# Mamba scan with a hand-written slot order: the z projection, its SiLU and a pooled product change slots

## The chip, the cores and the metric

The kernel runs on one core of a Trainium2 chip. The metric is the device time of one execution in microseconds (us). A core has five engines that run side by side, each with its own queue of instructions that it takes strictly in order: TensorE (PE in the profile: matrix products), VectorE (DVE), ScalarE (ACT: activation functions and copies), GpSimd (POOL) and SyncE (SP: here it only issues DMA transfers). They wait for one another through semaphores, so an instruction that waits also holds up everything that stands behind it on its engine.

## The reference

The kernel computes two layers over 4096 tokens of 256 channels: a convolution with attention, then a layer of a bidirectional Mamba, a small MLP and a mixture of experts. The change is in the Mamba. For each direction:

```
xz = einsum('bld,ed->ble', x, in_proj_w);  xc, z = split(xz, 2)
xc = silu(causal_conv(xc, K=4) + conv_b)
dt, B, C = split(xc @ x_proj_w)                 # 16, 16, 16
dt = softplus(dt @ dt_proj_w + dt_proj_b)
h[t] = exp(dt[t]*A) * h[t-1] + dt[t]*B[t]*xc[t]  # 512 channels x 16 states
y[t] = sum_states(h[t] * C[t]) + xc[t]*Dp
y = (y * silu(z)) @ out_proj_w
```

The two directions are added; then come a layer norm, an MLP with leaky ReLU and a second layer norm (in the kernel: the "tail").

## The kernel before

All four phases are in one program; the function `mamba_phase` holds the one at issue. Tokens are cut into 8 chunks of 512 (`NCH`), and each chunk is done in both directions: 16 iterations `i`, even ones forward, odd ones backward. `ET` = 4 blocks of 128 inner channels, and within each block the 16 states are four groups `k`, with 128 partitions holding 32 channels times 4 states. Two such tiles of 512 tokens make one slot (128 x 1024), so an iteration has 4 x 4 x 2 = 32 slots; `at` is the slot's number in it.

The order of every engine's instructions is the order in which the loop over `slots` at the end of `mamba_phase` emits them (`tc.manual_schedule`). Nothing is moved later. In slot n the loop emits:

- `inflow(n + 2)`: GpSimd multiplies dt*xc by B (L1928, tile `dbx`, three buffers). Its operands `dtxr` and `b` are spread over the partitions by DMAs that SyncE issues (`load_dt`, `load_bc`).
- `keep(n - 1)`: ScalarE copies the last column of slot n-1's scan into the state (L1977).
- `decay(n + 1)`: ScalarE computes exp(dt*A) into PSUM (L1918, tile `da`, two buffers), from the DMA'd tile `dtr`.
- `bring(n + 1)`: the carry, one column added to `dbx` (L1971 on ScalarE; in the slots of `LONG` L1969 on GpSimd). From iteration 2 on alone.
- `recur(n)`: VectorE's scan (L1941), in place in `da`, or into the tile `h` (four buffers) in the slots of `POOLED`.
- the product with C: by VectorE from `da` into `h` (`readout`, L1951), or, for a slot in `POOLED`, by GpSimd in place in `h`, emitted one slot later (`pooled`, L1956). Both follow the state's copy.
- `sum_states`: TensorE sums the states of two slots into `y` (L1986). It is emitted two slots after the pair's first one, or three where that is pooled. `h` of slot n is overwritten in slot n + 4, so this sum must be done by then.
- at slots 1, 9, 17 and 25 `close`: VectorE multiplies `y` by silu(z) (L1995).

Beside this the loop takes steps of generators, each a piece of other work between two `yield`s. `prepare(q)` makes the inputs of the next iteration, one step a slot: projections (slots 27 to 31), convolution as four tap products a block (slots 3 to 7), SiLU (slot 8), x projection `wx` (slot 9), dt projection `wdt` (slots 11 to 15), and softplus with a rounding term that TensorE adds up (`rounding`, `total`, `logs`, `keep_dt`; slots 17 to 26). The z half of the input projection is in it: `z_of` is two matrix products into one of two PSUM tiles `mm`, `keep_z` ScalarE's copy out of it. `output` is the output projection (slots 1 to 3). `tail(c)` is the layer norm, MLP and second layer norm of a finished chunk, whose 36 steps are taken in slots from 3 of an even iteration on; each step says which engine it needs next, and `FULL` names the slots in which that engine takes no step of the tail. Its layer norms pass a row through DMAs twice each, with SyncE waiting for the first before it issues the second (L138/L140 and L145/L146). Before the change the tail ends in slot 30 of the odd iteration.

SiLU is in another table of ScalarE than exp and log, so each SiLU has a table load before and after it.

Of the kernel before, what the change touches and what calls it, by code (L numbers as in the profile page):

```python
# [30 lines left out]
NCH = NT // N  # L31
# [6 lines left out]
ET = DI // P  # L38
# [1217 lines left out]
def mamba_phase(cx, early, w_in, w_x, w_out, w1, w2, x1d, ud, bcd, dtd, x2d, u2d, usum):  # L1256
# [12 lines left out]
    with ExitStack() as ctx:  # L1269
# [60 lines left out]
        def exp_and_log():  # L1330
            nc.scalar.preload_act_table_set("natural_log_exp_and_others")

        def mm_psum():
            return pmm.tile([P, N], FP, name="mm", tag="mm")
# [13 lines left out]
        def load_u(i):  # L1348
            c, d = divmod(i, 2)
            u = early.new_u()  # L1350
            nc.sync.dma_start(out=u, in_=ud[NCH - 1 - c if d else c])
            gots[i] = {"u": u}

        def in_pair(q, e):
            return [in_proj(q % 2, gots[q]["u"], e), in_proj(q % 2, gots[q]["u"], e + 1)]

        def few():
            return sp.tile([P, N], FP, name="few", tag="few", bufs=3)

        def prepare(q):  # L1360

            d, got = q % 2, gots[q]

            ps = in_pair(q, 0)
            yield
            yield
            xp = early.wide("xp")
            nc.scalar.copy(xp[:, :, 0:3], halo[d])
            for v in range(2):
                nc.scalar.copy(xp[:, v, 3:], ps[v])  # L1370
            ps = in_pair(q, 2)
            yield
            yield
            for v in range(2):
                nc.scalar.copy(xp[:, 2 + v, 3:], ps[v])
            nc.scalar.copy(halo[d], xp[:, :, N : N + 3])
            for _ in range(4):
                yield

            xc = None  # L1380
            for e in range(ET + 1):
                if e > 0:
                    xc = got["xc"] = xc or pr.tile([P, ET, N], FP, name="xc", tag="xc")
                    nc.scalar.activation(xc[:, e - 1, :], ps, AF.Identity, bias=cx.col(f"convb{d}", e - 1))
                if e < ET:
                    ps = mm_psum()
                    for k in range(4):
                        nc.tensor.matmul(  # L1388
                            ps, taps[d][:, 4 * e + k, :], xp[:, e, k : k + N], start=k == 0, stop=k == 3
                        )  # L1390
                yield
            nc.scalar.activation(xc, xc, AF.Silu)
            exp_and_log()
            yield
            ps = mm_psum()
            nx = DR + 2 * DS
            for e in range(ET):
                nc.tensor.matmul(ps[0:nx, :], wx[d][:, e, :], xc[:, e, :], start=e == 0, stop=e == ET - 1)
            z_of(q, 0)
            yield  # L1400
            xd = few()[0:nx, :]
            nc.scalar.copy(xd, ps[0:nx, :])
            keep_z(q, 0)
            z_of(q, 1)

            at = 0 if d else DR
            nc.sync.dma_start(out=bcd[q], in_=xd[at : at + 2 * DS, :])
            yield


            r = slice(32 * d, 32 * d + DR)
            ex = dt = None
            for e in range(ET + 1):
                if e == 0:
                    keep_z(q, 1)
                if e > 0:
                    ex = early.wide("ex")[:, :, 0:N] if e == 1 else ex
                    dt = got["dt"] = dt or sp.tile([P, ET, N], FP, name="dt", tag="dt")
                    nc.scalar.activation(ex[:, e - 1, :], ps, AF.Abs, bias=cx.col(f"dtb{d}", e - 1))
                    nc.scalar.activation(dt[:, e - 1, :], ps, AF.Relu, bias=cx.col(f"dtb{d}", e - 1))  # L1420
                if e < ET:
                    ps = mm_psum()
                    nc.tensor.matmul(ps, wdt[r, P * e : P * e + P], xd[r, :], start=True, stop=True)  # L1423
                yield

            nc.scalar.activation(ex, ex, AF.Exp, scale=-1.0)
            yield
            rds, sums = {}, {}

            def rounding(e):  # L1430
                rds[e] = few()
                nc.scalar.activation(rds[e], ex[:, e, :], AF.Identity, scale=-1.0, bias=-1.0)
                nc.scalar.add(rds[e], rds[e], 1.0)

            def total(e):
                sums[e] = mm_psum()
                for v, x in enumerate((rds.pop(e), ex[:, e, :], dt[:, e, :])):
                    nc.tensor.matmul(sums[e], cx.ident, x, start=v == 0, stop=False)  # L1438

            def logs(e):  # L1440
                nc.scalar.activation(ex[:, e, :], ex[:, e, :], AF.Ln, bias=1.0)

            def keep_dt(e):
                nc.scalar.copy(dt[:, e, :], sums[e])
                if q < 2:
                    return
                h = e // 2
                if e % 2 == 0:
                    firsts[q, h] = ip.tile([P, 2], FP, name="first", tag="first")
                nc.scalar.copy(firsts[q, h][:, e % 2 : e % 2 + 1], sums[e][:, 0:1])  # L1450
                if e % 2:
                    first_rows[q, h] = cx.rows.tile([P, 2], FP, name="first_row", tag="first_row", bufs=2)
                    nc.sync.dma_start(out=first_rows[q, h], in_=firsts[q, h])

            rounding(0)
            yield
            for e in range(ET + 1):
                if e > 0:
                    keep_dt(e - 1)
                if e < ET:  # L1460
                    total(e)
                if e < ET - 1:
                    rounding(e + 1)
                if 0 < e < 3:
                    keep_z(q, e + 1)
                yield
                if e < ET:
                    logs(e)
                    if e < 2:
                        z_of(q, e + 2)  # L1470
                    nc.tensor.matmul(sums[e], cx.ident, ex[:, e, :], start=False, stop=True)
                if e > 0:
                    dt_piece(q, 1, e - 1)
                if e == 1 and q + 1 < 2 * NCH:
                    load_u(q + 1)
                if e == ET and q > 1:
                    load_first(q, 0)
                yield

        def z_of(q, e):  # L1480
            zs[e] = in_proj(q % 2, gots[q]["u"], ET + e)

        def keep_z(q, e):
            if e % 2 == 0:
                gots[q].setdefault("z", []).append(sp.tile([P, 2, N], FP, name="z", tag="z", bufs=3))
            nc.scalar.copy(gots[q]["z"][e // 2][:, e % 2, :], zs.pop(e))
# [421 lines left out]
        gots, bcs, dts, m_of, das, us, ys, hs = {}, {}, {}, {}, {}, {}, {}, {}  # L1908
# [25 lines left out]
        def recur(n):  # L1934
# [3 lines left out]
            h = hs[n] = hp.tile([P, 2, N], FP, name="h", tag="h")  # L1938
            if n % SPS in POOLED:
                das[n] = h  # L1940
# [5 lines left out]
        def readout(n):  # L1946


            i, e, k, j = slots[n]
            if n % SPS not in POOLED:  # L1950
                nc.vector.tensor_tensor(hs[n], das[n], bcs[i, k][1][:, None, :].to_broadcast([P, 2, N]), ALU.mult)  # L1951

        def pooled(n):

            i, e, k, j = slots[n]
            nc.gpsimd.tensor_tensor(hs[n], hs[n], bcs[i, k][1][:, None, :].to_broadcast([P, 2, N]), ALU.mult)  # L1956
# [36 lines left out]
        def close(i, e):  # L1993
# [4 lines left out]
        CARRY = {30: (0, 0), 31: (0, 2), 9: (1, 0), 11: (1, 2)}  # L1998


        POOLED = {0, 4, 8, 12, 16, 20, 28}

        AHEAD = 5

# [1 line left out]
        LONG = {1, 9, 17, 24}  # L2006

        FULL = {
            "PE": {1, 2, 3, 4, 5, 6, 7, 9, 18, 20, 21, 22, 24, 27, 29},
            "ACT": {0, 6, 7, 8, 9, 14, 15, 16, 20, 22, 30, 31},  # L2010
            "POOL": {1, 5, 9, 13, 17, 21, 23, 25, 27, 29, 30, 31},
            "DVE": {8, 11, 16, 24},
            "DMA": {},
        }
        needs = ["PE"]
        with tc.manual_schedule(engines=ORDERED):
# [5 lines left out]
            for n, (i, e, k, j) in enumerate(slots):  # L2022
                at = n % SPS
# [12 lines left out]
                if nxt[0] < 2 * NCH:  # L2036
# [4 lines left out]
                    if (k, j) == (2, 2):  # L2041
                        load_dt(*nxt, 2)
                if n > 0 and (n - 1) % SPS in POOLED:
                    pooled(n - 1)
                if j == 2 and n > 2 and (n - 3) % SPS in POOLED:
                    sum_states(n - 3)
                if j == 0 and n > 0:
                    if (n - 2) % SPS not in POOLED:
                        sum_states(n - 2)
# [4 lines left out]
                if 1 <= at <= 3 and out is not None:  # L2054
                    step(out)
                    if at == 3:
                        out = None
                        if (i - 1) % 2:
                            tails.append(tail((i - 1) // 2))
                if at == 0 and i > 0:  # L2060
                    for z in gots[i]["z"]:
                        nc.scalar.activation(z, z, AF.Silu)
                    exp_and_log()
                if i == 0:
# [376 lines left out]
```

## Time and profile before

| what | value |
|---|---|
| median of 3 runs | 4107.07 us (4106.33 to 4110.94) |
| the profiled execution, its span | 4108.35 us, 4106.5 us |
| Mamba, start of iterations 2 and 14 | 2168.7 and 3584.2 us: 117.95 us an iteration |
| VectorE's scans, pooled ones, products (L1941, L1941, L1951) | 400 x 2347 ns, 112 x 2343 ns, 400 x 1221 ns |
| GpSimd's inflow and pooled products (L1928, L1956) | 512 x 2358 ns, 112 x 2357 ns |
| ScalarE's decay (L1918) | 1024 x 691 ns |
| z copy (L1486), z SiLU (L2062), a table load | 567, 1049, 1283 ns |
| mean granted TensorE clock | 0.935 |

A row of the profile's groups names the line, engine, operation and tiles (out<-in), how many there were, their busy time and mean duration, and then how long the engine sat idle before them and what ended that. In the view of waits a line reads "who <- for whom: total us, times, longest". In the timeline a row has its start, its length, the instruction and, in brackets, the idle time before it and its releaser. Instructions start a little before the one ahead has ended, so a plain slot takes VectorE 3.53 us and a pooled one 2.26.

### The profile page before, as it was taken

Reading aid. Unit: us, or ns where it says so; the run is one execution under the profiler, and the core shown is the slowest. Engines: PE = TensorE matmul, PEld = TensorE weight load, DVE = VectorE, ACT = ScalarE, POOL = GpSimd, SP = SyncE. Lnnn points to the kernel's source line nnn. Section 1 sums busy time; section 2 is a strip of 40 time slices with the busy share of each in tenths; the row PEclk is TensorE's granted clock in tenths of the full one; section 3 lists DMA queues with packets and bytes.
Section 4 is the critical chain, followed back from the end, with each engine's and each line's share of the span. In section 5 each row is a group of like instructions: output and inputs, shape, how many; then the busy total and the mean of one; then the engine's idle time right before and its main releaser. Section 6 shows DMA issues by size and latency. Waiting matters only on the chain. (4 is left out here: it accounts for less than half of the span.)

```text
span 4106.5 us, 43589 instructions
## 1 busy us (share of the span) xinstructions
PE 3577.7 (87%) x14968; PEld 1200.4 (29%) x14968; DVE 3456.2 (84%) x2887; ACT 2640.9 (64%) x4233; POOL 1814.7 (44%) x1193
## 2 busy tenths in 40 slices
PE   6769888999999999997788888888888988786898
PEld 2224332222222222222222223222322323222344
DVE  8998777989889889877899999998999999899322
ACT  1111226888888888875678777787877778775222
POOL 3020000000000000002888888888888889898100
PEclk9889998999999999998889999898999989897999
DMA  6232215223222323214333344434334334432121
GB/s 208 94 103 92 80 58 158 51 61 64 66 61 57 66 63 65 50 41 143 121 101 117 113 132 121 136 121 122 109 103 136 122 124 132 132 113 88 56 63 55
DMA packets 164325, 399.95 MB, mean 97 GB/s; under 512 B 36997, under 2 KB 46469, under 8 KB 163838
## 3 DMA queue, kind: packets, MB, share of 16 engines
q1 hardware_dynamic: 137166, 304.26, 23.9%
q0 software_dynamic: 24624, 84.43, 8.9%
q10 hardware_dynamic: 2304, 8.39, 0.6%
q8 instruction: 119, 1.95, 0.2%
q14 instruction: 112, 0.92, 0.1%
HBM read 268.17 MB, written 79.56 MB: 85 GB/s over the span
## 5 line engine op out<-in xcount | busy, mean ns | idle before, releaser
L1928 POOL TENSOR_TENSOR dbx<-dtxr,b 128x1024 f32<-128x1024 f32 x512 | 1202.6, 2358 | 225.5 <-DMA dtxr<-dtd 99.5
L1044 ACT ACTIVATE e<-sc 128x1024 f32<-128x1024 f32 x1024 | 993.7, 1023 | 165.5 <-PE sc L1037 143.0
L1941 DVE TENSOR_TENSOR_SCAN da<-da,state,dbx 128x1024 f32<-128x1024 f32 x400 | 938.9, 2347 | 58.5 <-ACT dbx L1971 17.4
L954 DVE TENSOR_TENSOR s<-s,e 128x1024 f32<-128x1024 f32 x768 | 880.2, 1216 | 19.7 <-ACT e L1044 19.0
L1918 ACT ACTIVATE da<-dtr,aneg 128x512 f32<-128x512 f32 x1024 | 707.9, 691 | 34.5 <-DMA dtr<-dtd 3.1
L1037 PE MATMUL sc<-q,kS 32*128 32x512 f32 x4096 | 648.7, 646 | 15.7 <-ACT e L1044 11.4
L961 PE MATMUL av<-e,vT 128*32 128x512 f32 x4096 | 551.8, 609 | 0.1
L1951 DVE TENSOR_TENSOR h<-da,c 128x1024 f32<-128x1024 f32 x400 | 488.5, 1221 | 22.9 <-PE mm L1423 1.4
L977 POOL DMA_DIRECT2D s<-s x94 | 81.5, 874 | 942.3 <-DVE s L954 856.8
L462 PE MATMUL cv<-v,u 128*128 128x512 f32 x928 | 413.5, 606 | 28.3 <-DVE pad L283 14.2
L1986 PE MATMUL y<-h,sel 128*32 128x512 f32 x2048 | 335.8, 629 | 95.0 <-DVE h L1951 77.2
L1037 PEld LDWEIGHTS sc<-q,kS 32*128 32x128 f32 x4096 | 211.0, 184 | 455.8 <-issue 254.0
L1941 DVE TENSOR_TENSOR_SCAN h<-da,state,dbx 128x1024 f32<-128x1024 f32 x112 | 262.5, 2343 | 53.6 <-PE y L1986 44.1
L1956 POOL TENSOR_TENSOR h<-h,c 128x1024 f32<-128x1024 f32 x112 | 263.9, 2357 | 28.9 <-ACT state L1977 28.8
L1342 PE MATMUL mm<-u,win 128*128 128x512 f32 x464 | 237.7, 654 | 30.7 <-ACT xp L1370 28.1
L462 PEld LDWEIGHTS cv<-v,u 128*128 128x128 f32 x928 | 179.1, 195 | 260.5 <-issue 228.1
L560 DVE SCALAR_TENSOR_TENSOR acc<-pad,wdw_s,acc 128x768 f32<-128x768 f32 (+1 forms) x192 | 235.9, 1233 | 19.9 <-ACT acc L553 14.2
L1977 ACT COPY state<-da 128x2 f32<-128x2 f32 x399 | 63.1, 158 | 280.8 <-DVE h L1951 279.4
L1388 PE MATMUL mm<-xp,taps 128*128 128x512 f32 x480 | 214.1, 598 | 0.0
L143 POOL TENSOR_TENSOR ln_few<-ln_few,minus_half 128x4 f32<-128x4 f32 x29 | 32.1, 1106 | 398.4 <-DMA ln_few<-ln_row 259.5
L954 DVE TENSOR_TENSOR s<-e 128x1024 f32<-128x1024 f32 x128 | 152.0, 1217 | 59.2 <-ACT e L1044 50.3
L961 PEld LDWEIGHTS av<-e,vT 128*32 128x32 f32 x4096 | 81.7, 108 | 394.4 <-issue 386.7
(381 smaller groups left out, 3910.8 us busy)
## 6 DMA issues: line engine op xcount, KB each, us to landing
dtr<-dtd SPq DMA_DIRECT2D x128, 512.0 KB
dtxr<-dtd SPq DMA_DIRECT2D x128, 512.0 KB
s<-s POOLq DMA_DIRECT2D x94, 512.0 KB, 6.0
b<-bcd SPq DMA_DIRECT2D x64, 256.0 KB
c<-bcd SPq DMA_DIRECT2D x64, 256.0 KB
dtd<-dt SPq DMA_DIRECT2D x64, 256.0 KB
dtd<-few SPq DMA_DIRECT2D x64, 256.0 KB
u<-uv SPq DMA_DIRECT2D x24, 640.0 KB
```

The costliest lines, as they stand in the source:

```text
L462: nc.tensor.matmul(rows4(ps), u[:, dy, P * ci : P * ci + P], v[:, dy : dy + HR, ci, :], start=dy + ci == 0, stop=dy == k - 1 and ci == CT - 1,
L954: nc.vector.tensor_tensor(z, x, y, ALU.add)
L961: nc.tensor.matmul(g.av[32 * h : 32 * h + 32, :], vT[:, kb, P * t + 32 * h : P * t + 32 * h + 32], es[h // 2][:, h % 2, :], start=kb == 0, ...
L1037: nc.tensor.matmul(ps[h // 2][:, h % 2, :], kS[r, t, P * kb : P * kb + P], q_t[r, t, :], start=True, stop=True,)
L1044: nc.scalar.activation(e, ps[i], AF.Exp)
L1342: nc.tensor.matmul(ps, win[d][:, t, P * e : P * e + P], u[:, t, ::-1] if d else u[:, t, :], start=t == 0, stop=t == CT - 1,)
L1918: nc.scalar.activation(da[:, v, :], dts[i, e, j][0][:, v, :], AF.Exp, scale=aneg[i % 2][:, a : a + 1])
L1928: nc.gpsimd.tensor_tensor(u, dts[i, e, j][1], bcs[i, k][0][:, None, :].to_broadcast([P, 2, N]), ALU.mult)
L1941: nc.vector.tensor_tensor_scan(das[n].rearrange("p v n -> p (v n)"), da.rearrange("p v n -> p (v n)"), u.rearrange("p v n -> p (v n)"), st ...
L1951: nc.vector.tensor_tensor(hs[n], das[n], bcs[i, k][1][:, None, :].to_broadcast([P, 2, N]), ALU.mult)
L1956: nc.gpsimd.tensor_tensor(hs[n], hs[n], bcs[i, k][1][:, None, :].to_broadcast([P, 2, N]), ALU.mult)
L1986: nc.tensor.matmul(ys[i, e][32 * j : 32 * j + 32, :], cx.sel, hs[n + j // 2][:, j % 2, :], start=False, stop=k == SQ - 1,)
```

## The change

The z products go from slots 9, 10, 19 and 21 to slots 15, 17, 19 and 21, the copies of them from slots 10, 11, 20 and 22 to slots 17, 18, 21 and 23, and the SiLU of z from slot 0 of the iteration that uses it to slot 28 of the one before. The rounding term of block 2 goes from slot 20 to 19. Slot 0's product with C goes to VectorE and slot 10's to GpSimd. The sets `FULL` change, which moves the steps of the tail: it now begins in slot 11 instead of 8, and ends in slot 4 of the next even iteration.

```
             for e in range(ET):
                 nc.tensor.matmul(ps[0:nx, :], wx[d][:, e, :], xc[:, e, :], start=e == 0, stop=e == ET - 1)
-            z_of(q, 0)
             yield
             xd = few()[0:nx, :]
             nc.scalar.copy(xd, ps[0:nx, :])
-            keep_z(q, 0)
-            z_of(q, 1)
...
-                if e == 0:
-                    keep_z(q, 1)
...
                     nc.tensor.matmul(ps, wdt[r, P * e : P * e + P], xd[r, :], start=True, stop=True)
+                else:
+                    z_of(q, 0)
                 yield
...
             rounding(0)
+            keep_z(q, 0)
+            z_of(q, 1)
             yield
...
-                if e < ET - 1:
+                if e == 0 or e == 2:
                     rounding(e + 1)
-                if 0 < e < 3:
-                    keep_z(q, e + 1)
+                if e == 0:
+                    keep_z(q, 1)
                 yield
                 if e < ET:
                     logs(e)
+                    if 0 < e < 3:
+                        keep_z(q, e + 1)
                     if e < 2:
                         z_of(q, e + 2)
                     nc.tensor.matmul(sums[e], cx.ident, ex[:, e, :], start=False, stop=True)
+                if e == 0:
+                    rounding(2)
...
-        POOLED = {0, 4, 8, 12, 16, 20, 28}
+        POOLED = {4, 8, 10, 12, 16, 20, 28}
...
-            "PE": {1, 2, 3, 4, 5, 6, 7, 9, 18, 20, 21, 22, 24, 27, 29},
-            "ACT": {0, 6, 7, 8, 9, 14, 15, 16, 20, 22, 30, 31},
-            "POOL": {1, 5, 9, 13, 17, 21, 23, 25, 27, 29, 30, 31},
-            "DVE": {8, 11, 16, 24},
+            "PE": {1, 2, 3, 4, 5, 6, 7, 8, 9, 10, 15, 18, 19, 20, 21, 22, 24, 27, 29},
+            "ACT": {6, 7, 8, 9, 16, 17, 18, 19, 22, 28, 29, 31},
+            "POOL": {5, 9, 11, 13, 17, 21, 23, 25, 27, 29, 30, 31},
+            "DVE": {1, 9, 11, 17, 25},
...
-                if at == 0 and i > 0:
-                    for z in gots[i]["z"]:
+                if at == 28 and i + 1 < 2 * NCH:
+                    for z in gots[i + 1]["z"]:
                         nc.scalar.activation(z, z, AF.Silu)
                     exp_and_log()
```

Where the steps of the tail stand, by iteration and slot (e: even, o: the odd one after, E: the even one after that):

| step | before | after |
|---|---|---|
| mean product, subtraction, square | e8, e9, e10 | e11, e12, e13 |
| row out (L138/L140), power and row back (L143 to L146) | e12, e15 | e15, e18 |
| residual sum L1581, copies of m L1578 | e13/e14, e14 and e17 | e16/e17, e17 and e20 |
| normalization L149 on GpSimd, scale L1584 | e19, e21 | e22, e23 |
| MLP, L1594 to L1600 (products on VectorE) | e25, e28, e30, o8 | e28, e31, o11, o13 |
| MLP, L1605 and L1610 | o8, o10, o12 | o13, o16, o23 |
| second norm: subtraction, square | o13, o17 | o24, o25 |
| second norm: row out, power and row back | o21, o24 | o27, E0 |
| second norm: normalization L149, sum L1617 | o28, o29 | E3, E4 |

## The prediction

> **What bounds it now.** First the page: the profiled execution took 4108.35 us around a span of 4106.5, 1.3 us over the median of the runs shown.
>
> ```profile
> PE 3577.7 (87%) x14968; PEld 1200.4 (29%) x14968; DVE 3456.2 (84%) x2887; ACT 2640.9 (64%) x4233; POOL 1814.7 (44%) x1193
> ```
>
> Shares over the whole span mix four phases, so I then cut the Mamba phase into its iterations, an odd and an even one shown here (columns: stretch, us, then busy time of PE, PEld, DVE, ACT, POOL):
>
> ```profile
> 2755.00:2877.40 122.40, 99.93 (x288) 34.13 (x288) 109.66 (x68) 88.92 (x182) 101.75 (x58) 0.90 0.39 119
> 2877.40:2992.50 115.10, 100.38 (x296) 34.55 (x296) 109.34 (x69) 91.42 (x186) 101.04 (x58) 0.96 0.43 124
> ```
>
> VectorE works 109.5 us in each; what is left is its waiting. An odd iteration and the even one take 14.25 us of it, from the view of VectorE's waits over iterations 2 to 13 (six pairs):
>
> ```profile
> DVE h L1941 <- PE y L1986: 35.4, 18, 5.9
> DVE da L1941 <- ACT dbx L1971: 17.4, 18, 1.8
> DVE da L1941 <- ACT state L1977: 11.5, 11, 1.8
> DVE da L1941 <- POOL dbx L1969: 8.1, 5, 2.6
> DVE usum L1617 <- POOL u L149: 5.5, 6, 1.7
> ```
>
> So the change can save 14 us a pair at most. Third, the timeline tells where those waits sit. I write s8 for slot 8 and put its zero at the start of its scan. In s0 ScalarE's z SiLU holds up the decay of s2:
>
> ```profile
> 2756.75 1.28 ACT L2062 ACT_TABLE_LOAD   x1
> 2758.05 2.00 ACT L2062 ACTIVATE z<-z 128x1024 f32<-128x1024 f32 x2
> 2760.07 1.28 ACT L1331 ACT_TABLE_LOAD   x1
> ...
> 2761.46 1.41 ACT L1918 ACTIVATE da<-dtr,aneg 128x512 f32<-128x512 f32 x2
> 2762.81 0.28 ACT L1971 ACTIVATE dbx<-dbx,brought 128x1 f32<-128x1 f32 x1
> ```
>
> From load to carry's end it is 6.37 us, while s0 and s1 give VectorE 6.5 (2.26 pooled, 3.53 plain, 0.59 for the gate L1995). The worst stall is s12 of odd iterations: its scan overwrites the tile that TensorE must first sum for s8, and that sum stands behind two z projections and the tail's L1605 products:
>
> ```profile
> 2795.64 3.70 PE L1342 MATMUL mm<-u,win 128*128 128x512 f32 x8
> 2799.18 1.88 PE L1605 MATMUL tl<-a1a,w2s 128*128 128x512 f32 x4
> 2800.89 1.88 PE L1605 MATMUL tl<-a1b,w2s 128*128 128x512 f32 x4
> ...
> 2803.56 1.06 PE L1986 MATMUL y<-h,sel 128*32 128x512 f32 x8
> ```
> ```profile
> 2804.73 2.35 DVE L1941 TENSOR_TENSOR_SCAN h<-da,state,dbx 128x1024 f32<-128x1024 f32 x1 [5.88 <-PE y L1986]
> ```
>
> Last, TensorE after idling. The same 128x512 half-products that start every 0.43 us in the rows above start every 0.85 here:
>
> ```profile
> 2941.31 2.08 PE L1438 MATMUL mm<-few,ident 128*128 128x512 f32 x2 [5.21 <-ACT few L1433]
> 2943.18 1.91 PE L1438 MATMUL mm<-ex,ident 128*128 128x512 f32 x2
> ```
>
> **The change part by part.** No operation is added or dropped: VectorE keeps 25 products of 1.22 and 32 scans of 2.35 an iteration, GpSimd 7 products of 2.36. All is in the waits, so I rebuild them by stretch, per pair.
>
> *s8 to s16: z projections and copies leave s9 to s11; s10 becomes pooled.* ScalarE in s8: keep and decay of s9 end at 1.7, two table loads and the 1.91 us SiLU at 6.2, keep of s8, decay and carry of s10 at 8.0. VectorE is there after 2.26 + 3.53 + 0.59 = 6.4: s10 waits 1.64. Today the tail's sums cover part of that (0.73 at s8 in odd, 1.21 at s9 in even iterations); the new FULL sets move them to s11 and s12. TensorE then runs wx from 4.9 to at most 10.5 (half speed), skip 0.9, sum of s8 0.9: done 12.3, and s12 is due at 13.8, so **the wait at s12 goes**. GpSimd: its carry step waited 4.06 us on ScalarE, itself behind the z copy; now it runs at 11.5, then the input of s13 to 13.9, the new product of s10 to 16.2, input of s14 to 18.6, s15 to 21.0, product of s12 to 23.3, input of s16 to 25.7. Due: s13 16.1, s14 19.6, s16 26.6. Covered, by a microsecond only at s14 and s16. At s8 itself the even wait goes (the sum reduction, now in s4, gives TensorE 1.14 more); in odd iterations s0 to s2 lose today's waits, four tap products of 3.45 us finish late, and s8 waits 0.65. Waits: even 1.65, odd 2.25. Today 0.49 + 0.58 + 2.01 + 0.11 = 3.2 in each on average.
>
> *s28 to s3: the z SiLU.* The same chain starts 1.95 after s28: the carry of s30 ends at 1.95 + 6.37 = 8.32, VectorE is ready at 2.26 + 3.53 = 5.79, or 6.43 where the tail puts a 0.73 product in s28 (even). So s30 waits 2.53 odd and 1.89 even: it is the old stall of s2 in a new place, and larger, since s1 had the 0.59 gate. At s0 nothing is pooled or loaded any more, so s1 and s2 lose their 0.67 and 1.19, and the reduction's 0.46 wait on GpSimd at s29 goes (it stands after GpSimd's normalization in s4). One new debt: SyncE's dtr load of s29 waits for the decay of s30, now at 8.0 instead of about 5.0, and dtxr queues behind it. Issue at 9.1, 5.5 us to the data where few transfers are under way (s21 of iteration 7), 8.7 at this boundary in iteration 3: it lands between 14.6 and 17.9, the input of s1 is ready 2.6 later, and VectorE asks at 18.9 (odd) or 19.5. Waits from 0 to 1.6; I take 0.3 after odd and 0 after even iterations, since part of that delay is backlog which now drains while SyncE waits. Waits: 1.89 + 2.53 + 0.3 = 4.7 a pair; today 2.3 an iteration.
>
> *s17 to s25: z copies behind the rounding terms.* The rounding pair is 1.27, a copy 0.57. In odd iterations z's second projection and the tail keep TensorE busy until the sums begin, and s13, s16, s23, s24 carry tail work on VectorE; TensorE ends the sum of s16 11.5 after s17, which s20 wants at 11.1, and ScalarE stays ahead of s21 to s25: 0.4 to 0.5 in place of about 1.9 (0.56 at s20, 0.75 at s22, 0.74 at s24 in iteration 7). In even ones the tail's residual sum (L1581) now needs a copy of m that stands in s17 after rounding and z copy: ScalarE ends it 5.1 after s17. TensorE has been idle since 2.2, so the four half-products start slow: 3.6, then the total (0.85 + 5 x 0.43 = 3.0), skip and sum of s16 1.8: 13.6 against 11.0 at which s20 is due. **A new wait of about 2.5 at s20**; had TensorE stayed fast, 0.3. From there ScalarE is the chain: beside its 1.8 a slot for state, decay and carry it has the third rounding and logs in s22 and s23 behind the copy of dt, which waits for TensorE's z product, which waits for the z copy of s21. It ends dt's copy 24.1 after s17, rounding 25.3, the decay of s24 26.8, due 26.5; then logs 0.6, z copy 0.6 and the tail's scale 1.5 put the carry of s25 at 31.1, due 30.4. So 0.4 at s24 and 0.7 at s25. Even 3.6, today about 0.9.
>
> *Tail and its transfers.* The tail now crosses into s4 of the next even iteration; two blocking pairs of DMAs (a row out and back, 2.7 to 3.7 us each on SyncE) move from s12/s15 to s15/s18 and from s21/s24 to s27/s0. At s27 the 3.5 us are over before the load of s29 may start anyway; at s0 the next load is needed 12 us later. Nothing, then; up to 1.0 a pair if not.
>
> *Sum per pair:* 1.65 + 2.25 + 4.7 + 0.5 + 3.6 = 12.7, against 14.25: 1.55 less. Seven pairs, 10.9 us; iterations 0 and 1, with no tail, I hold even. 4108.35 - 10.9 - 1.3 for the median: **4096 us**.
>
> [...] In this trace 11 of 14 gaps of 2.0 to 3.0 us are followed by products at half pace (2.29 us before the L1605 product at 2786.83). [...]
>
> **Rivals.**
> *Faster, 4070 to 4090.* TensorE stays fast at s17 and the ScalarE load of s19 to s25 fits: 12.7 - 2.2 - 1.1 = 9.4 a pair, 34 us less than now, 4073. For it: the z projections fill time in which TensorE was idle. Against: the gaps above.
> *Slower, 4111 to 4120.* The SiLU in s28 delays the dtr/dtxr pair, and s1 waits for it in every iteration. It begins at a landing 16.3 after s28 (odd) or 16.9 (even), that is 7.2 and 7.8 after issue; in iterations 3 and 7 it took 8.7 and 7.8. Each microsecond beyond costs two a pair. At 8.7: 1.5 odd, 0.9 even, less the 0.3 counted, 2.1 a pair, 15 us: 4111. Since b and c of s28 now stand right ahead of it instead of 3 us earlier, 9.4 is possible: 3.5 a pair, 24 us: 4120. For it: SyncE's waits on ScalarE; against: nothing else is issued while SyncE waits, so the backlog drains.
> *GpSimd falls behind* at s14 or s16, with three products in s8, s10 and s12: its margins there are 1.0 and 0.9. In s14 of iteration 7 it waited 0.55 for dtxr; 2 to 3 us of such waits an iteration cost 1 to 2, 14 to 28 in all, from 4110 to 4124.
> *No change:* waits only change place; 4099 to 4115.
>
> **Numbers.** Noise is about 0.2%, 8 us. Chances: the sum above with a gain that can be told, 4085 to 4099, 0.30; faster rival 0.17; no change 0.15; slower by transfers 0.22; by GpSimd or an unlisted wait, 0.16. Bounds: the best of all terms is 9 a pair (4070), the worst adds longer half pace (0.6), late transfers (3.5) and a stall as large as today's at s12 (4.0): 20.8 a pair, 4153. A waits-only sum can also miss by a microsecond or two a pair either way, so I reach to 4062 below and, giving up the case of all ills at once, to 4140 above; the likeliest case alone spans 4085 to 4105.
>
> **What would show it.** Right: VectorE busy 109.5 still; s12's wait on L1986 near zero; a wait of 1.9 to 2.5 on ScalarE before s30; 1.0 to 1.7 before s10 in every iteration; about 2.5 on L1986 before s20 in even iterations alone. Wrong: a wait on GpSimd before s1 over 1 us, or GpSimd waiting for dtxr past the start of s0; waits at s13 to s16; the row of TensorE at s17 at full pace.

## The result, and the profile after

The changed kernel takes 4134.60 us (median of 4 runs, 4127.74 to 4138.24) against 4109.00 us before: a ratio of 1.0061, 95% interval 1.0043 to 1.0078. It is slower, by 25 us. The forecast was 4096 us, 11 us faster. The profiled execution took 4132.73 us around a span of 4130.9, 24.4 us more than that of before.

The page's line of engine totals of the changed kernel shows the same amount of work on VectorE (3456.6 against 3456.2 us):

```profile
PE 3606.7 (87%) x14968; PEld 1198.1 (29%) x14968; DVE 3456.6 (84%) x2887; ACT 2643.6 (64%) x4233; POOL 1820.7 (44%) x1193
```

The stretches of an odd and an even iteration of the changed kernel (the columns are those of the prediction's table: stretch, length, busy time of PE, PEld, DVE, ACT, POOL, clock, DMA share, GB/s):

```profile
2769.95:2887.86 117.91, 100.20 (x306) 33.83 (x300) 108.69 (x67) 90.59 (x185) 97.50 (x56) 0.94 0.36 115
2887.86:3008.83 120.97, 102.25 (x284) 33.62 (x284) 110.33 (x69) 90.47 (x184) 103.28 (x59) 0.89 0.40 122
```

The odd iteration got shorter (122.40 to 117.91 us), the even one longer (115.10 to 120.97); the pair went from 237.5 to 238.9 us here, and over iterations 2 to 13 from 117.95 to 119.39 us an iteration. VectorE is as busy as before, so all of this is waiting. Its waits in iterations 2 to 13 of the changed kernel (total us, times, longest; its lines stand three further down, so the scan is L1944, the carry L1974, the decay L1921 and the sum L1989):

```profile
DVE da L1944 <- ACT dbx L1974: 47.7, 30, 2.4
DVE h L1944 <- ACT state L1980: 19.0, 12, 1.7
DVE h L1944 <- PE y L1989: 17.0, 7, 2.6
DVE da L1944 <- ACT da L1921: 9.2, 6, 1.5
DVE m L1564 <- PE mm L1557: 5.9, 6, 1.0
DVE ln_xc L129 <- PE tl L122: 4.1, 12, 0.4
```

With two lines of 0.8 us together that is 103.7 us, 17.3 a pair, against 14.25 before and 12.7 forecast. Three more a pair, six times, are 18 of the 24 us that the two profiled executions differ by. Iterations 14 and 15 add 2.0, and 0 and 1 take 2.6 less: the Mamba phase, from its first scan to its last, is 17 us longer. The other 8 us lie ahead of it and behind it, where nothing was edited; over the twelve traces of this case the last activation of the attention ends between 1879 and 1893 us. The waits on TensorE's sums have halved (35.4 to 17.0); those on ScalarE's carries (`dbx`) went from 17.4 to 47.7, 30 times in place of 18. Eighteen of the 30 were in the forecast: s30 in every iteration and s25 in the even ones. The other twelve are s5 and s21 of the odd iterations, 1.70 us each, and with them go six waits of 1.54 us on a decay (`da` L1921), at s17 of the even ones. (Before, VectorE also waited six times for a decay, but 0.7 us, and at s24 of odd iterations.)

What holds ScalarE up there stands in the page's own groups. The decay's row, first before, then after (busy, mean ns, idle time of ScalarE in front of it, and what ended most of that):

```profile
L1918 ACT ACTIVATE da<-dtr,aneg 128x512 f32<-128x512 f32 x1024 | 707.9, 691 | 34.5 <-DMA dtr<-dtd 3.1
```
```profile
L1921 ACT ACTIVATE da<-dtr,aneg 128x512 f32<-128x512 f32 x1024 | 708.2, 692 | 74.6 <-DVE h L1944 43.5
```

ScalarE's decays now wait 43.5 us for a scan of VectorE, the scan of a pooled slot. The timeline of ScalarE at s16 to s18 of iteration 8 shows one of these waits:

```profile
2947.08 0.16 ACT L1980 COPY state<-da 128x2 f32<-128x2 f32 x1
2949.39 1.42 ACT L1921 ACTIVATE da<-dtr,aneg 128x512 f32<-128x512 f32 x2 [2.15 <-DVE h L1944]
2950.74 1.90 ACT L1423 ACTIVATE ex<-ex 128x2048 f32<-128x2048 f32 x1
...
2955.80 0.59 ACT L1581 COPY m<-tl 128x512 f32<-128x512 f32 x1
```

and VectorE's timeline in the same place:

```profile
2947.01 2.35 DVE L1944 TENSOR_TENSOR_SCAN h<-da,state,dbx 128x1024 f32<-128x1024 f32 x1
2950.89 2.36 DVE L1944 TENSOR_TENSOR_SCAN da<-da,state,dbx 128x1024 f32<-128x1024 f32 x1 [1.54 <-ACT da L1921]
```

The decay of s17 starts when the scan of s16 ends (2947.01 + 2.35 = 2949.36), not a slot ahead of it. VectorE must then wait out the whole decay: 1.42 us, or 1.70 where the carry (0.28) follows on ScalarE. The decay of s21 in iteration 7, where the carry is on ScalarE, and the scan that waits for it:

```profile
2843.42 1.42 ACT L1921 ACTIVATE da<-dtr,aneg 128x512 f32<-128x512 f32 x2 [2.10 <-DVE h L1944]
```
```profile
2845.08 2.36 DVE L1944 TENSOR_TENSOR_SCAN da<-da,state,dbx 128x1024 f32<-128x1024 f32 x1 [1.70 <-ACT dbx L1974]
```

That is what happens when a slot and the one before it have the same buffer. The two built programs list the PSUM bank of every tile, and there it stands: `da` has two buffers, and they are not handed out by turns. In the changed program s17 of even iterations and s5 and s21 of odd ones get the buffer of the slot directly before, in iterations 2 to 14 (7 times s17, 6 times s5 and s21), and so do five slots of iteration 0; in the program of before that happens in iteration 0 alone (s9, s13, s17). All of these slots follow a pooled one.

### The profile page after: what moved, and what is told of

Read it like the earlier page. It is cut to its first block, busy times and chain, and to the rows that moved or that the text cites. A ratio compares the mean times of both kernels' runs of the same rounds, so it can differ in the third digit from the quotient of the medians.

```text
span 4130.9 us, 43570 instructions
## 1 busy us (share of the span) xinstructions
PE 3606.7 (87%) x14968; PEld 1198.1 (29%) x14968; DVE 3456.6 (84%) x2887; ACT 2643.6 (64%) x4233; POOL 1820.7 (44%) x1193
## 5 line engine op out<-in xcount | busy, mean ns | idle before, releaser
L1944 DVE TENSOR_TENSOR_SCAN da<-da,state,dbx 128x1024 f32<-128x1024 f32 x400 | 939.0, 2348 | 79.1 <-ACT dbx L1974 48.1
L1921 ACT ACTIVATE da<-dtr,aneg 128x512 f32<-128x512 f32 x1024 | 708.2, 692 | 74.6 <-DVE h L1944 43.5
L1989 PE MATMUL y<-h,sel 128*32 128x512 f32 x2048 | 309.0, 637 | 35.5 <-POOL h L1959 21.5
L1342 PE MATMUL mm<-u,win 128*128 128x512 f32 x464 | 254.8, 689 | 92.8 <-ACT xp L1370 84.4
L1944 DVE TENSOR_TENSOR_SCAN h<-da,state,dbx 128x1024 f32<-128x1024 f32 x112 | 262.5, 2344 | 44.3 <-PE y L1989 21.7
L143 POOL TENSOR_TENSOR ln_few<-ln_few,minus_half 128x4 f32<-128x4 f32 x29 | 37.1, 1278 | 396.3 <-DMA ln_few<-ln_row 285.5
```

The lines of the kernel that those rows point to most:

```text
L1342: nc.tensor.matmul(ps, win[d][:, t, P * e : P * e + P], u[:, t, ::-1] if d else u[:, t, :], start=t == 0, stop=t == CT - 1,)
L1921: nc.scalar.activation(da[:, v, :], dts[i, e, j][0][:, v, :], AF.Exp, scale=aneg[i % 2][:, a : a + 1])
L1944: nc.vector.tensor_tensor_scan(das[n].rearrange("p v n -> p (v n)"), da.rearrange("p v n -> p (v n)"), u.rearrange("p v n -> p (v n)"), st ...
L1989: nc.tensor.matmul(ys[i, e][32 * j : 32 * j + 32, :], cx.sel, hs[n + j // 2][:, j % 2, :], start=False, stop=k == SQ - 1,)
```

## The experiments

The first theory: the shared buffers cost the three waits, and most of what follows them; without them the change gains about what was forecast. Rivals: the waits come from the moved work itself (ScalarE has too much to do in s17), or from the SiLU in s28, or from TensorE's half pace alone. Times on different chips are compared through the ratio to the kernel before on the same chip; 0.001 of it is 4.1 us.

**The buffers by turns, in the changed kernel and in the kernel before.** Two tags of one buffer each in place of one tag of two (two more tiles, outside the slots, get one of the two tags):

```
-        pda = ctx.enter_context(tc.tile_pool(name="c_pda", bufs=2, space=PSUM))
+        pda = ctx.enter_context(tc.tile_pool(name="c_pda", bufs=1, space=PSUM))
...
-            da = das[n] = pda.tile([P, 2, N], FP, name="da", tag="da")
+            da = das[n] = pda.tile([P, 2, N], FP, name="da", tag=f"da{n % 2}")
```

> The changed kernel with one edit: the tile da, in two buffers of one tag, becomes two tags of one buffer, taken in turn by even and odd slots. In the changed kernel the decays of s17 (even), s5 and s21 (odd) were given the PSUM buffer of the slot just before them, so that they had to wait for that slot's scan; in the kernel before this happens in iteration 0 alone. Theory: these three waits (1.54 + 1.70 + 1.70 = 4.94 us a pair of iterations) are what the prediction missed; they go, nothing else moves, and seven pairs give 35 us: about 4100 us, a ratio of 0.997 to 0.999 to before. Rival: ScalarE is late in these slots anyway (it has 3.3 to 3.9 us of work in each of s13 to s15); then the waits stay at 1 us or more and the time at 4125 to 4135.

> The kernel before with the same edit. It had shared buffers at s9, s13 and s17 of iteration 0 alone. Theory: no more than 0 to 4 us faster, 4103 to 4109 us. Rival, that taking turns by itself helps every iteration: over 10 us faster.

Measured: the changed kernel with buffers by turns 4095.28 us, ratio 0.9957 (0.9942 to 0.9973); the kernel before with them 4112.96 us, 0.9997 (0.9982 to 1.0013). So the edit is worth 0.0104, 43 us, in the one and nothing that can be told in the other. In the first, the decay's row and VectorE's waits of iterations 2 to 13 read:

```profile
L1921 ACT ACTIVATE da<-dtr,aneg 128x512 f32<-128x512 f32 x1024 | 708.2, 692 | 32.8 <-DMA dtr<-dtd 3.2
```
```profile
DVE da L1944 <- ACT dbx L1974: 27.3, 18, 2.4
DVE h L1944 <- ACT state L1980: 15.4, 12, 1.5
DVE h L1944 <- PE y L1989: 15.2, 13, 2.2
```

The idle time on the scan is gone, and so are the waits at s5, s17 and s21: 18 carries are left, and no wait on a decay. All waits come to 66.3 us, 11.05 a pair. The wait of s20 in even iterations fell too, from 2.65 to 0.53 us in five of six; a new one of 1.52 us came at s8 in odd iterations. The scan of s20 in iteration 8, in the changed kernel and with buffers by turns:

```profile
2964.66 2.35 DVE L1944 TENSOR_TENSOR_SCAN h<-da,state,dbx 128x1024 f32<-128x1024 f32 x1 [2.65 <-PE y L1989]
```
```profile
2946.35 2.35 DVE L1944 TENSOR_TENSOR_SCAN h<-da,state,dbx 128x1024 f32<-128x1024 f32 x1 [0.53 <-PE y L1989]
```

The theory stands, and against the rivals: the moved work and the SiLU in s28 are all still there, and the three waits are gone.

**TensorE's half pace at s17.** In the changed kernel TensorE idles there until ScalarE's copy of m (2955.80 above), and then works at half pace (two half-products take 1.88 in place of 1.12 us; the trace's record of the granted clock has 0.5 from 0.23 us after their start on, for 3.41 us):

```profile
2956.44 1.88 PE L1584 MATMUL tl<-m,ident 128*128 128x512 f32 x2 [3.01 <-ACT m L1581]
2958.12 1.91 PE L1585 MATMUL tl<-x,ident 128*128 128x512 f32 x2
2959.83 1.16 PE L1435 MATMUL mm<-few,ident 128*128 128x512 f32 x2
```

To see what that costs by itself, the z product of s17 is issued twice in even iterations, which fills 1.7 us of the idle time. The first run has that on top of the buffers by turns, the second on the changed kernel as it is:

```
             z_of(q, 1)
+            if d:
+                for t in range(CT):
+                    nc.tensor.matmul(
+                        zs[1], win[d][:, t, P * (ET + 1) : P * (ET + 2)], gots[q]["u"][:, t, ::-1],
+                        start=t == 0, stop=t == CT - 1,
+                    )
             yield
```

> The first kernel with, in even iterations, the second z product issued twice (the same result written again), which fills 1.7 of the 3.0 us in which TensorE idles in s17. Theory, that the wait before s20 of even iterations (2.65) comes from half-pace products after that gap: the residual sum and the total run at full pace, the wait falls to 0.3 to 0.6, 14 to 16 us in seven pairs. Rival, that the order alone makes it (the copy of m ends 5.1 after s17 and 6 us of work stand ahead of the sum of s16): it stays over 2 us and the time within 4 us of the first kernel.

> The changed kernel with its shared buffers left as they are, and the second z product of s16 issued twice in even iterations, so that TensorE has no 3.0 us gap before the third one at s17. The output is as before. If half pace after that gap makes the wait of s20 (the 3.0 us gap in the profile, then matmuls of 1.03 to 1.06 us), the wait of s20 in even iterations goes from 2.65 us to 0.3 to 0.8 us, and the time from 4134.6 us to 4117 to 4122 us (8 even iterations by some 2 us). If the third product is late because ScalarE frees its input late (the shared buffer at s17), whatever TensorE's pace, the wait stays above 2 us and the time within 5 us of 4134.6.

Measured: on top of the buffers by turns 4088.49 us, 0.9944 (0.9921 to 0.9967), which can't be told from 0.9957: with the buffers by turns alone the gap was already 1.1 to 1.7 us in five of six even iterations, and the pace full, so there was little to win. On the changed kernel 4118.45 us, 1.0020 (1.0005 to 1.0035), against 1.0061: 17 us, the time that the clock's theory had. (Lines behind 1454 stand six further down in both.) In iteration 8 of that run the gap is shorter and the products run at full pace, though ScalarE is held up at s17 as before:

```profile
2947.42 1.13 PE L1590 MATMUL tl<-m,ident 128*128 128x512 f32 x2 [2.58 <-ACT state L1986]
2948.38 1.02 PE L1591 MATMUL tl<-x,ident 128*128 128x512 f32 x2
```
```profile
2953.93 2.35 DVE L1950 TENSOR_TENSOR_SCAN h<-da,state,dbx 128x1024 f32<-128x1024 f32 x1 [0.95 <-PE y L1995]
```

s20 waits 0.95 in four of six even iterations. In the other two the gap was 2.89 us; the products began at full pace, the granted clock fell to half 1.2 and 1.4 us later, and s20 waited 2.65 again. So TensorE's pace at s17 costs 17 us by the medians; the Mamba phases of the two traces differ by 11.

What the shared buffers cost as a whole adds up from the waits in iterations 2 to 13. The changed kernel waits 17.3 us a pair, the one with buffers by turns 11.05. Of these 6.2, 4.94 are the three waits, 1.8 the wait of s20, 0.6 that of s10 in odd iterations and 0.4 the tail's subtraction, and the wait of s8 takes back 1.5. Six pairs make 37 us; the Mamba phases of the two traces differ by 41, the medians by 43.

**The SiLU back in slot 0**, with the buffers by turns:

```
-                if at == 28 and i + 1 < 2 * NCH:
-                    for z in gots[i + 1]["z"]:
+                if at == 0 and i > 0:
+                    for z in gots[i]["z"]:
```

> The first kernel of this call with the z SiLU back in slot 0 of the iteration that uses it. Theory (a stall is the ScalarE chain less VectorE's work in two slots): the waits before s30 (2.41 odd, 1.75 even) go; in s0, which is no longer pooled, VectorE has 3.53 + 3.53 + 0.59 = 7.65 against a chain that ends at 1.7 + 6.37 = 8.1 to 8.3, so s2 waits 0.4 to 0.7. About 1.5 us an iteration less, 22 us: 4075 to 4082. Rival: the stall of 2 us simply comes back at s2, as before the change (1.2 to 1.8): within 8 us of the first kernel.

Measured: 4071.49 us, 0.9891 (0.9864 to 0.9918). It beats both kernels, by somewhat more than expected, and no version measured is clearly faster. The 0.0066 to the version with the SiLU in s28 is 27 us; the Mamba phases of the two traces differ by 15. VectorE's largest waits in it are

```profile
DVE h L1944 <- ACT state L1980: 16.4, 13, 1.6
DVE da L1944 <- POOL dbx L1972: 11.5, 7, 3.4
DVE h L1944 <- PE y L1989: 10.4, 11, 2.2
```

The wait of s30 is gone; s1 now waits 0.96 us an iteration for GpSimd and s2 0.54 for ScalarE. With a product for VectorE to do in slot 0, the chain of SiLU and decay is nearly covered there: 56.7 us of waits in iterations 2 to 13 against 66.3. That is 1.6 a pair, so the waits explain less than half of the 27.

**The SiLU in slot 28 as the only part of the change**, in the kernel before with buffers by turns (the diff above in reverse).

> The kernel before with the two buffers of da by turns, and of the change only this: the SiLU of z in slot 28 of the iteration before in place of slot 0. Theory: the wait at s2 (1.38 us an iteration) goes, and one of about 2 us comes at s30, because ScalarE's 2.6 us of SiLU and of loading its table stand before the products of s29 and s30, which gives 0.3 to 0.6 us an iteration and a time of 4115 to 4122 us against 4113 us without the edit. Rival: ScalarE has less to do in s28 to s30 without the other moves of the change, the wait at s30 is under 1 us, and the edit by itself gains, 4100 us or less.

Measured: 4133.30 us, 1.0061 (1.0043 to 1.0078). The sign is the theory's, the size is three times the most that it allowed (9 us): 0.0064 over the control, 26 us, as much as in the changed kernel. (The Mamba phases of the two traces differ by 14 us.) Waits of iterations 2 to 13 in it:

```profile
DVE h L1941 <- PE y L1986: 56.8, 30, 4.3
DVE da L1941 <- ACT dbx L1971: 19.6, 21, 1.8
```

In the control they are 34.2 and 17.0. The wait at s30 is 1.11 us an iteration, less than expected; but VectorE now waits 0.76 at s0 and 1.37 at s8 for TensorE's sums (0 and 0.19 in the control). At s0 it is the SiLU again: ScalarE's copy of `xp` stands behind it, TensorE waits for that copy, and then takes 6.63 us for eight products of the projection, which took 3.60 in the control, ahead of the sum that s0 needs (iteration 6, before s0 of iteration 7):

```profile
2756.42 6.63 PE L1342 MATMUL mm<-u,win 128*128 128x512 f32 x8 [3.90 <-ACT xp L1370]
```

At s8 VectorE, no longer held at s1 and s2, comes before the sum is there. What was won at s1 and s2 (1.77 to 0.37) is waited for again at s0 and s8.

**Slot 10's product in place of slot 0's as the only part**, in the same control.

```
-        POOLED = {0, 4, 8, 12, 16, 20, 28}
+        POOLED = {4, 8, 10, 12, 16, 20, 28}
```

> The kernel before with the two buffers of da by turns, and of the change only this: slot 10's product on GpSimd in place of slot 0's. First theory: the waits of s1 and s2 of before (0.39 and 1.38 us an iteration) mostly go, since s0 and s1 then take 7.64 us against a chain of about 8.1 us, and the wait at s12 or s10 grows by some 1.3 us in the odd iterations, which leaves about 1.3 us a pair, and a time of about 4100 us against 4113 us without the edit. Rival: what is won at s1 and s2 is all waited for again at s10 to s12, and the time stays at 4108 to 4118 us.

Measured: 4128.83 us, 1.0047 (1.0032 to 1.0062): slower by 20 us than the control (17 in the Mamba phases of the traces), which neither theory had. s1 and s2 gave back 1.2 us an iteration, as expected; but s12 of odd iterations waits 7.09 us (3.65 in the control). TensorE and VectorE at s9 to s12 of iteration 7 in it:

```profile
2799.13 2.85 PE L1605 MATMUL tl<-a1a,w2s 128*128 128x512 f32 x4 [2.29 <-DVE a1b L1600]
2801.77 2.75 PE L1605 MATMUL tl<-a1b,w2s 128*128 128x512 f32 x4
...
2808.02 3.70 PE L1342 MATMUL mm<-u,win 128*128 128x512 f32 x8
```
```profile
2817.11 2.35 DVE L1941 TENSOR_TENSOR_SCAN h<-da,state,dbx 128x1024 f32<-128x1024 f32 x1 [7.09 <-PE y L1986]
```

VectorE now asks for s12 1.1 us sooner after s10, and TensorE is later: behind a gap of 2.29 us (1.85 in the control) the eight L1605 products run at a lower pace, 5.4 us for 3.7.

**The z products, rounding terms, copies and the tail's places alone**: buffers by turns, SiLU in slot 0, slot 0's product on GpSimd again (the two diffs above).

> The changed kernel with da by turns, the SiLU of z in slot 0 and slot 0's product on GpSimd, both as before: of the change only the places of the z products, the rounding terms and the copies are left. First theory: the parts act on each other; the exchange of slots 0 and 10 alone cost 16 us because VectorE waits longer at s12, where TensorE's queue of s11 is the bound, and with the z products out of that stretch there is no wait at s12, so that the exchange gains its 0.4 to 1.3 us an iteration at s1 and s2: without it the time is 4078 to 4092 us, against 4071.5 us with it. Second theory: the parts simply add, and without the exchange the time is 4071.5 less 16, about 4055 us.

Measured: 4091.25 us, 0.9957 (0.9944 to 0.9970), at the upper end of the first theory's range. Beside the version with the exchange of products (0.9891) the exchange is worth 27 us here; alone it cost 0.0050 over the control, 20 us. (In the Mamba phases of the traces it is 20 gained here and 17 lost alone.) The parts act on each other: with the z products out of s9 to s11 there is no wait at s12, so the time that the exchange frees at s1 and s2 is kept.

**The shared buffers alone, in the kernel before**, at the slots where the changed kernel has them (and in iteration 15), on top of the two tags above:

```
+        def flips(n):
+
+            i, at = divmod(n, SPS)
+            turns = [x for x in range(2, i)] if i > 2 else []
+            done = sum(2 if x % 2 else 1 for x in turns)
+            if i > 1:
+                done += (at > 4) + (at > 20) if i % 2 else at > 16
+            return done
...
-            da = das[n] = pda.tile([P, 2, N], FP, name="da", tag="da")
+            da = das[n] = pda.tile([P, 2, N], FP, name="da", tag=f"da{(n + flips(n)) % 2}")
```

> The kernel before with the two buffers of da by turns, except that slot 17 of even iterations and slots 5 and 21 of odd iterations are given the same buffer as the slot directly before, from iteration 2 on: the pattern that the changed kernel has, and nothing else of the change. If the shared buffer is what costs, whatever work lies around it, VectorE waits some 1.5 to 1.7 us at each of the three (4.9 us a pair), and the time goes from 4113 us to 4130 to 4145 us. Rival: the kernel before has slack in ScalarE's work at these slots, the sharing alone costs less than 8 us, and the cost in the changed kernel comes from the sharing and the moved work together.

Measured: 4169.31 us, 1.0155 (1.0126 to 1.0184), 65 us over the control and twice the most that was expected. The three waits are 1.70, 1.54 and 1.70 us, to the hundredth those of the changed kernel, and the decay's row shows it as there (lines nine further down than before):

```profile
L1927 ACT ACTIVATE da<-dtr,aneg 128x512 f32<-128x512 f32 x1024 | 707.8, 691 | 84.1 <-DVE h L1950 51.5
```

The three are 4.94 us a pair, and s12 of odd iterations waits 6.6 us for 4.0 on the average; smaller waits fall by about 1. Waits in iterations 2 to 13 come to 6.5 us a pair more than in the control, and the Mamba phases of the two traces differ by 46 us. The rest of the 65 is not found in the traces. TensorE at s8 and s9 of iteration 7 in it:

```profile
2800.18 1.05 PE L1995 MATMUL y<-h,sel 128*32 128x512 f32 x4 [1.33 <-DVE h L1960]
2803.08 3.78 PE L1605 MATMUL tl<-a1a,w2s 128*128 128x512 f32 x4 [1.85 <-DVE a1b L1600]
2806.65 3.20 PE L1605 MATMUL tl<-a1b,w2s 128*128 128x512 f32 x4
```

In the control the same eight products take 1.99 + 1.88 us after a gap of the same 1.85; here a gap of 1.33 stands shortly before it, and they run at half pace.

**Slot 6's product in place of slot 8's**, on the version with the SiLU back in slot 0, since it waits for ScalarE at s10:

```
-        POOLED = {4, 8, 10, 12, 16, 20, 28}
+        POOLED = {4, 6, 10, 12, 16, 20, 28}
```

> The changed kernel with da by turns and the SiLU of z in slot 0, and slot 6's product on GpSimd in place of slot 8's. Theory: VectorE then takes 7.64 us for s8 and s9 in place of 6.4 us, against a chain on the other engines of about 8.0 us, so that the wait of s10 (1.34 us an iteration) falls to 0.1 to 0.5 us and that of s8 in odd iterations is smaller; time 4050 to 4056 us against 4071.5 us. Rival: with two products of s4 to s7 on GpSimd, TensorE's or ScalarE's chain there (s4 to s7 then take 1.3 us less on VectorE) becomes the bound, the wait moves to s6 to s8, and the time stays within 8 us of 4071.5 us, or is longer.

Measured: 4078.14 us, 0.9932 (0.9911 to 0.9954): not faster than 0.9891, and by the intervals not clearly slower. The rival holds. The wait at s8 went, but s10 still waits 1.52 us an iteration and s7 now 0.23.

## Why the prediction was wrong

The parts one behind the other, by the ratios to the control (buffers by turns, 0.9997): z products, rounding, copies and the tail's places -16 us; the exchange of products -27 behind them (+20 alone); the SiLU in s28 +27; the buffers as they were handed out +43. Together +26, from 0.9997 to 1.0061. By the intervals each such difference is sure to some 8 to 13 us only. The Mamba phases of the profiled executions, one of each, give the same signs: -17, -20 (+17 alone), +15 and +41. Without the last part the change would gain, by the ratio 18 us where 11 were forecast.

**The step that failed** is "ScalarE stays ahead of s21 to s25", and with it the silent one that ScalarE is ahead at s5 and s17. The working had the decays run a slot ahead of their scans, as they can when `da`'s two buffers alternate. They do alternate in the kernel before from iteration 2 on, and do not in the changed one. The waits themselves cost 1.54 + 1.70 + 1.70 = 4.94 us a pair, with what follows from them 6.2, and the prediction has no term for it. Taken out, the time is 4095.28 us, where 4096 was forecast.

**That agreement is in part luck.** The waits that are left are 11.05 us a pair where 12.7 were forecast, and single terms miss both ways. At s20 a wait of "about 2.5" was forecast and 2.65 measured, but the cause was the shared buffer. The working had TensorE idle from 2.2 us after s17 to the copy of m at 5.1. With buffers by turns the copy is where it was put (s17 at 2934.72, the copy's end at 2939.79: 5.07), but TensorE is busy until 4.0:

```profile
2936.86 1.88 PE L1342 MATMUL mm<-u,win 128*128 128x512 f32 x4
2939.84 1.12 PE L1584 MATMUL tl<-m,ident 128*128 128x512 f32 x2 [1.09 <-ACT state L1980]
```

The gap is 1.09, not 2.9, the pace full, and s20 waits 0.53, as in four more of the six even iterations. "Had TensorE stayed fast, 0.3" was the nearer number. Against that, s8 in odd iterations waits 1.52 where 0.65 was put down (in the changed kernel VectorE, held 1.70 at s5, comes there too late to wait), and s20 in odd ones does not wait where 0.4 to 0.5 was put down.

**What held.** *s30:* 1.89 and 2.53 forecast, 1.75 and 2.41 measured in every iteration of the changed kernel. ScalarE's chain in s28 to s30 and the scan that waits for it:

```profile
2874.30 1.28 ACT L2065 ACT_TABLE_LOAD   x1
2875.59 2.00 ACT L2065 ACTIVATE z<-z 128x1024 f32<-128x1024 f32 x2
2877.61 1.28 ACT L1331 ACT_TABLE_LOAD   x1
...
2880.35 0.28 ACT L1974 ACTIVATE dbx<-dbx,brought 128x1 f32<-128x1 f32 x1
```
```profile
2880.66 2.36 DVE L1944 TENSOR_TENSOR_SCAN da<-da,state,dbx 128x1024 f32<-128x1024 f32 x1 [2.41 <-ACT dbx L1974]
```

*s10:* 1.64 forecast, 1.1 to 1.7 measured. *s12:* the stall is gone. TensorE ends the sum for it 13.4 us after s8 (forecast 12.3), and the scan starts without a wait at 14.3:

```profile
2804.36 6.37 PE L1398 MATMUL mm<-xc,wx 128*48 128x512 f32 x8 [3.81 <-ACT xc L1392]
2810.66 1.12 PE L1987 MATMUL y<-xc,skip 128*128 128x512 f32 x2
2811.72 1.06 PE L1989 MATMUL y<-h,sel 128*32 128x512 f32 x8
```
```profile
2813.66 2.34 DVE L1944 TENSOR_TENSOR_SCAN h<-da,state,dbx 128x1024 f32<-128x1024 f32 x1
```

*Transfers and GpSimd:* s1 waits for GpSimd once in twelve iterations, 0.3 us, and there is no wait on it at s13 to s16. Both slower rivals were unfounded; the slower side came from "an unlisted wait". *Smaller misses:* s25 0.40 for 0.7, s24 in even iterations none for 0.4; the addition to `m` at s3 of even iterations waits 0.97 for TensorE, and the tail's subtraction up to 0.4, neither in the sum. Two small sums of its opening are off without weight: the rows from load to carry's end make 6.34 us, not 6.37, and 2.26 + 3.53 + 0.59 is 6.38, not 6.5.

**The gaps of TensorE.** The forecast took the half pace at s17 from the gaps of 2.0 to 3.0 us in the trace of before. At s17 of the changed kernel the gaps of 3.01 to 3.33 us were all followed by half pace, so that reading was right. The prediction's own count, 11 of 14 gaps, does not come out of the trace: in iterations 2 to 13 of the kernel before, 22 gaps in front of TensorE are 2.0 to 3.0 us long, and after 19 of them the granted clock was at half within 2 us. The reading stands, the count does not.

## What to carry to other kernels

When a hand-made order of instructions changes, look up in the built program which buffer each tile gets before and after: a pool of two buffers that alternates in one order may hand the same one out twice running in another, and the row to look at is the idle time in front of the producer, ended by its own consumer. Where it matters, give each buffer a tag of its own. And judge the parts of a change on top of the others, not alone: a product exchange that cost 20 us by itself gained 27 once the wait behind it had been taken away.

## What was not expected of the hardware

In these traces TensorE's half pace makes more of small delays, and the length of the last gap alone does not tell where it follows. At s17 of even iterations gaps of 3.01 to 3.33 us were all followed by it in the changed kernel. With the z product issued twice there, the pace after a gap of 2.58 us in iteration 8 was full (1.13 and 1.02 us for two half-products each); after 2.89 us in iteration 2 the first two took 1.12 us and the third pair 1.91. At s9 of iteration 7 the control kept full pace after a gap of 1.85 us; with the buffers shared the same gap, with one of 1.33 us shortly before it, was followed by half pace, and the scan of s12 waited 6.73 us, 3.08 more than in the control.

What goes with a fall shows in the record of the granted clock beside TensorE's busy time. In the traces of before and after it is 1.0 or 0.5, and its changes lie a multiple of 3.41 us apart, to within 0.03 us. Cut into stretches of that length between the points of change, iterations 2 to 13 of the two have 59 stretches at full clock in which the trace has TensorE busy for a share under 0.39, and the clock fell to half after all 59 (23 before, 36 after). With a share over 0.45 it fell after 7 of 643; why after those few is open. For the two gaps of 1.85 us an estimate from the rows agrees: in the 3.41 us up to the gap's end TensorE was busy 1.05 us with the buffers shared, a share of 0.31, and 1.56 us in the control, 0.46. No run was made to test this.

By which rule the two buffers of `da` are handed out was not traced; that the shared ones all follow a pooled slot, whose scan frees its buffer sooner, is only an observation.
